# Moving a LayerNorm's 1/std broadcast within a hand-ordered state-space layer

## The chip, the cores and the metric

The kernel runs on one NeuronCore of a Trainium2 chip. The core has five engines that run side by side, each through its own list of instructions: TensorE (PE, matmuls and transposes), VectorE (DVE), ScalarE (ACT), GpSimd (POOL) and SyncE (SP, which here only issues DMAs). The metric is the device time of one execution in microseconds (us). Before the change it is 11733.97 us, the median of three runs (11728.79 to 11737.78).

## What is computed

The input is 4 images of 192 channels and 128 x 128 pixels. Layer 1 of the network (called `layer0` in the code) is a fractional-Fourier convolution block; the change does not touch it. Layer 2 (`layer1` in the code) is a GroupNorm followed by a selective state-space block over the 16384 pixels of each image as one sequence. Cut to what matters:

```python
mu  = jnp.mean(seq, -1, keepdims=True)                      # over the 192 channels of one token
var = jnp.mean(jnp.square(seq - mu), -1, keepdims=True)
seq = (seq - mu) * lax.rsqrt(var + LN_EPS) * ln_g + ln_b    # LayerNorm
xs, z = jnp.split(jnp.einsum('blc,ec->ble', seq, in_proj_w), 2, axis=-1)
u  = silu(causal depthwise conv(xs) + conv_b)
dt, Bm, Cm = jnp.split(jnp.einsum('bld,kd->blk', u, x_proj_w), ...)
dt = jax.nn.softplus(jnp.einsum('blr,dr->bld', dt, dt_proj_w) + dt_proj_b)
def step(hcar, inp):                                        # over tokens, 384 x 16 states
    hnew = hcar * jnp.exp(dt_t[..., None] * A) + (dt_t * u_t)[..., None] * B_t[:, None, :]
    y_t  = jnp.sum(hnew * C_t[:, None, :], axis=-1)
out = jnp.einsum('bld,cd->blc', (y + u * Dp) * silu(z), out_proj_w)
```

## The kernel before

**Tiling.** Layer 2 cuts the sequences into 128 chunks of 512 tokens. In a chunk the 384 inner channels are three blocks `j` of 128 partitions, and the 16 states of each are taken two at a time, so a chunk is 24 groups, `k = 0..23`, with `j = k // 8` and `sg = k % 8`. A group has two scans: one `tensor_tensor_scan` on VectorE (L868) runs the recurrence of one state over 512 tokens. Below, "scan 22.1" is the second scan of group 22.

**What a scan needs.** The decay `exp(dt*A)` comes from ScalarE (`da` or `op`, L799). The input `dt*u*B` comes from one of three places: from VectorE itself (`product`, L819), for some groups from GpSimd (`inputs`, L827: `db`), and for `sg == 6` from ScalarE and TensorE (`scale_pair` L843, then four transposes in `turned_back`, L854). GpSimd multiplies each group's result by C (`hc`, L881) and TensorE sums those into `py` (L894), three groups later (`LAG = 3`). At the end of a block `j`, ScalarE copies `py` out (`evacuate`, L903), TensorE turns it (`turn`, L918, four transposes into a PSUM tile `pf`), and VectorE multiplies by `silu(z)` (`gate`, L923, which writes `yg`).

**The front end of later chunks.** While the 24 groups of chunk n run, the generator `front(n + 2)` computes what a later chunk needs: GroupNorm and LayerNorm, `in_proj`, the convolution, silu, `x_proj`, softplus. It is started at group 14 of chunk n and advanced once per group, so two fronts are under way at a time. Each `yield` ends its work in that group. A bare `yield` resumes at the front's fixed place in the next group, ahead of the scans. `yield MID` hands the following piece to the list that is resumed between the two scans of the same group (`between`), and `yield LATE` to the list that is resumed after both.

**The part that is changed** is LayerNorm's scaling of `s`, the 192 x 512 values kept as `[96, 2, 512]`. The variance of the 512 tokens ends up as `rs`, 128 partitions x 4. ScalarE takes the root (L640), VectorE the reciprocal (L643, after the scans of group 20), TensorE turns `rs` into 4 rows (L646, group 21, a PSUM tile `rt`), ScalarE copies them to `rows` (L649, between the scans of group 21), four matmuls with the selector `sel` spread them over 96 partitions (L653, group 22, a PSUM tile `rb`), and VectorE multiplies `s` by that (L657, after the scans of group 22). `in_proj` of the scaled `s` (L663) begins in group 23.

**Order.** The whole layer is recorded under `tc.manual_schedule()`, so each engine executes in the order in which the code issues its instructions. Per group the order is: the finishing of the previous chunk, the gate, `turned_back`, `sums`, the fronts' step, `turn`, `inputs`, the scans with what stands between them, and then the late pieces. The groups concerned, on TensorE: group 20 has the sums, one `in_proj` of `z` for the older front (two matmuls, L663) and the turn; group 21 a `turned_back`, the sums, L646 and a second `turned_back`; group 22 the sums, another `in_proj` of `z`, L653; group 23 the sums and the first `in_proj` of the scaled `s`.

**Buffers.** The PSUM tiles of the fronts, of `turn` and of `turned` all come from one pool of three (`psum()`); a new tile waits until the last reader of the one whose place it takes is done. The `da` tiles come from a pool of four, `h` of three, `hc` of five, `db` of two.

```python
yield MID        # rows = copy(rt)            between the scans of group 21
yield            # rb: selector matmuls       at the front's place in group 22
yield LATE       # s *= rb                    after the scans of group 22
```

Of the kernel before, what the change touches and what calls it, by code (L numbers as in the profile page):

```python
# [42 lines left out]
def _bc(ap, axis, n):  # L43

    a = ap.unsqueeze(axis)
    shape = list(a.shape)
    shape[axis] = n
    return a.to_broadcast(shape)
# [455 lines left out]
def layer1(tc, xmid, out, st2, w, n_tok=S * S):  # L504
# [11 lines left out]
    MID, LATE = "mid", "late"  # L516
    with ExitStack() as ctx:
# [68 lines left out]
        def psum():  # L586
            return ps1.tile([128, 512], F32, name="ps")
# [6 lines left out]
        def load_x(i):  # L594
            b, ch = divmod(i, NCHUNK)
            xm = xp.tile([CH, 2, T], F32, name="xm")
            nc.sync.dma_start(
                out=xm, in_=xmid[b][:, ch * T : (ch + 1) * T].rearrange("(t p) f -> p t f", p=CH)
            )
            got[i]["xm"] = xm  # L600

        def front(i):
# [38 lines left out]
            yield  # L641
            yield LATE
            nc.vector.reciprocal(rs, rs)  # L643
            yield
            rt = psum()
            nc.tensor.transpose(rt[0:4, 0:128], rs, ident)  # L646
            yield MID
            rows = tp.tile([4, 128], F32, name="rows")
            nc.scalar.copy(rows, rt[0:4, 0:128])  # L649
            yield  # L650
            rb = psum()
            for q in range(4):
                nc.tensor.matmul(  # L653
                    rb[0:CH, q * 128 : (q + 1) * 128], sel[:, q, :], rows, start=True, stop=True
                )
            yield LATE
            nc.vector.tensor_tensor(s, s, _bc(rb[0:CH], 1, 2), ALU.mult)  # L657
            yield

# [110 lines left out]
        def load_bc(i, sg):  # L770

            t = bcp.tile([128, 2, G, T], F32, name="bc")
            nc.sync.dma_start(
                out=t, in_=got[i]["dbc"][:, sg * G : (sg + 1) * G, :].partition_broadcast(128)
            )
            got[i]["bc", sg] = t

        def dtu_copy(n, j):

            g = got[n]  # L780
            g["dp"] = psd.tile([128, T], F32, name="dp")
            nc.scalar.copy(g["dp"], g["dtu"][j])  # L782
# [19 lines left out]
        def early(i):  # L802

            if i < len(own):
                decay(own[i], scp.tile([128, T], F32, name="da"))

        def decay_there(s):

            if s < len(states) and s not in turns:
                decay(s, psa.tile([128, T], F32, name="op"))  # L810

        def product(s):


            if s in turns and states[s][1] % NG != BY_PE:
                n, k, q = states[s]
                g = got[n]
                dbs[s] = psa.tile([128, T], F32, name="op")
                nc.vector.tensor_tensor(dbs[s], g["dp"], g["bc", k % NG][:, 0, q, :], ALU.mult)  # L819

        def inputs(n, k):

            if by_pool(k):
                g = got[n]
                j, sg = divmod(k, NG)
                db = g["db", k] = scp.tile([128, G, T], F32, name="db", bufs=2)
                nc.gpsimd.tensor_tensor(db, _bc(g["dtu"][j], 1, G), g["bc", sg][:, 0], ALU.mult)  # L827
# [19 lines left out]
        def turned_back(at):  # L847

            if at < len(states) and states[at][1] % NG == BY_PE:
                n, k, q = states[at]  # L850
                db = dbs[at] = psa.tile([128, T], F32, name="op")
                t = got[n].pop(("dbT", k // NG, q))
                for blk in range(T // 128):
                    nc.tensor.transpose(db[:, blk * 128 : (blk + 1) * 128], t[:, blk, :], ident)  # L854
# [29 lines left out]
        def sums(n, k):  # L884

            g = got[n]
            j, sg = divmod(k, NG)
            if sg == 0:
                g["py", j] = psy.tile([128, T // 128, 128], F32, name="py")
            py, hc = g["py", j], g.pop(("hc", k))  # L890
            for q in range(G):
                for blk in range(T // 128):
                    first = sg == 0 and q == 0 and blk == 0
                    nc.tensor.matmul(  # L894
                        py[:, blk, :], hc[:, q, blk * 128 : (blk + 1) * 128], ident, start=first,
                        stop=sg == NG - 1 and q == G - 1 and blk == T // 128 - 1,
                        is_transpose=True, skip_group_check=True,
                    )

        def evacuate(n, j):  # L900
            g = got[n]
            yt = g["yt", j] = op.tile([128, T // 128, 128], F32, name="yt")
            nc.scalar.copy(yt, g["py", j])  # L903
# [16 lines left out]
        def gate(n, j):  # L920
            g = got[n]
            yg = g["yg", j] = op.tile([128, T], F32, name="yg", bufs=3)
            nc.vector.tensor_mul(yg, g["pf", j], g["zs"][j])  # L923
# [24 lines left out]
        def start_front(n):  # L948
            if n < total:
                fronts.append(front(n))  # L950

        def step(works, parts):

            for f in list(works):
                got_on = next(f, f)
                if got_on is f:
                    works.remove(f)
                elif got_on is not None:
                    parts[got_on].append(f)

        def go_on(fs):
            for f in fs:
                next(f, None)

        with tc.manual_schedule():
            for i in range(min(2, total)):
                load_x(i)
            for _ in front(0):
                pass
            for sg in range(NG):  # L970
                load_bc(0, sg)
            dtu_copy(0, 0)
            inputs(*order[1])
            for at in range(AHEAD):
                early(at)
            for s in range(2):
                product(s)
            decay_there(2)


            start_front(1)
            for _ in range(NGR - FRONT):
                parts = {MID: [], LATE: []}
                step(fronts, parts)
                go_on(parts[MID] + parts[LATE])
            tails = []
            for pos, (n, k) in enumerate(order):
                j, sg = divmod(k, NG)
                if k == FRONT:
                    start_front(n + 2)  # L990
                if k == NGR - 2 and n + 1 < total:
                    assert len(fronts) == 1 + (n + 2 < total), fronts
                parts = {MID: [], LATE: []}
                step(tails, parts)

                before = n - (j == 0), (j - 1) % NJ
                if pos >= NG and sg == LAG + 3:
                    gate(*before)
                if sg == BY_PE - 1:
                    turned_back(G * (pos + 1))  # L1000
                if pos >= LAG and sg != LAG:
                    sums(*order[pos - LAG])
                if k == EARLY or sg == LAG - 1 and j < NJ - 1:
                    turned(n, NJ - 1 if k == EARLY else j)
                if sg == NG - 3 and pos + 3 < len(order):
                    m, q = order[pos + 3]
                    dtu_copy(m, q // NG)
                step(fronts, parts)
                if pos >= NG and sg == LAG + 1:
                    turn(*before)  # L1010
                if pos + 2 < len(order):
                    inputs(*order[pos + 2])

                def between():
                    go_on(parts[MID])
                    if sg == LAG and j < NJ - 1:
                        scale_pair(n, j)

                scans(pos, n, k, between)
                if pos >= NG and sg == LAG - 1:  # L1020
                    evacuate(*before)
                go_on(parts[LATE])
                if k == EARLY:
                    scale_pair(n, NJ - 1)
                if pos >= LAG and sg == LAG:
                    sums(*order[pos - LAG])
                    add_skip(n, j)
                if k == LAG + 3 and n:
                    tails.append(finish(n - 1))
                if k == LAG + 8 and n + 2 < total:  # L1030
                    load_x(n + 2)
                if k >= NGR - BCL and n + 1 < total:
                    load_bc(n + 1, k - (NGR - BCL))
                if k < NG - BCL and n:
                    load_bc(n, k + BCL)
            for at in order[-LAG:]:
                sums(*at)
            evacuate(total - 1, NJ - 1)
            turn(total - 1, NJ - 1)
            gate(total - 1, NJ - 1)  # L1040
            for _ in finish(total - 1):
                pass
# [139 lines left out]
```

## Time and profile before

| what | value |
|---|---|
| median of three runs | 11733.97 us |
| the profiled execution | 11752.54 us, its span 11750.5 us |
| VectorE busy | 10759.5 us, 92% of the span |
| GpSimd busy | 10087.8 us, 86% |
| TensorE matmuls busy | 9994.0 us, 85% |
| ScalarE busy | 8606.6 us, 73% |
| L868, all scans | 6144 instructions of about 1271 ns |
| L657, scaling of s | 128 instructions of 1217 ns, 225.6 us idle before them |

The page of the profile has for each engine its busy time and its share of the span, then the same in 40 slices of the span, then the groups of instructions by source line: how many, how long one takes, and for how long the engine stood idle just before them and what ended that. Layer 2 begins about 1500 us into the span and takes the rest. The profiled execution is 18.6 us longer than the median of the plain runs, 0.16%.

### The profile page before, as it was taken

The page shows a single profiled execution, that of the slowest core. Times are in us where ns is not written, and L with a number is a line of the kernel's source. Part 1 is how long each engine was busy: PE and PEld are TensorE (multiplying, and loading weights), DVE is VectorE, ACT ScalarE, POOL GpSimd, SP SyncE. Part 2 cuts the span into 40 slices and gives each one's busy share as a digit, 9 for nine tenths or more (in the row PEclk, how much of TensorE's full clock was granted, in tenths as well). Part 3 has the DMA queues.
Part 4 walks back from the last instruction along what each step waited for, and adds up shares of the span by engine and source line. Part 5 has one row for each costly group of instructions (what it writes and reads, how often), then busy time and mean ns, then how long its engine had stood idle before and what let it go on. Part 6 is the DMA issues. An engine that isn't in the chain of part 4 may idle for free.

```text
span 11750.5 us, 153548 instructions
## 1 busy us (share of the span) xinstructions
PE 9994.0 (85%) x50570; PEld 6788.1 (58%) x50570; DVE 10759.5 (92%) x11584; ACT 8606.6 (73%) x14436; POOL 10087.8 (86%) x4598
## 2 busy tenths in 40 slices
PE   4777888888888888888888888888888888888887
PEld 2444456666666666666666666666666666666665
DVE  5565579999999999999999999999999999999999
ACT  2322178788888788788788788788888878878876
POOL 0000089999999999999999999999999999999999
PEclk8888689999999999999999999999999999999998
DMA  8887633433433443443443443443343343344343
GB/s 208 209 223 194 185 109 113 124 114 111 124 117 108 124 123 103 126 125 100 126 124 102 123 124 106 120 124 108 117 124 113 113 124 115 111 124 118 108 124 97
DMA packets 1339384, 1494.09 MB, mean 127 GB/s; under 512 B 903473, under 2 KB 954358, under 8 KB 1338070
## 3 DMA queue, kind: packets, MB, share of 16 engines
q1 hardware_dynamic: 1318102, 1421.34, 42.0%
q0 software_dynamic: 13312, 50.34, 1.3%
q10 hardware_dynamic: 7168, 12.59, 0.3%
q8 instruction: 398, 6.52, 0.2%
q14 instruction: 404, 3.31, 0.1%
HBM read 1325.19 MB, written 155.32 MB: 126 GB/s over the span
## 4 chain that ended last, share of the span: by engine, by line
DVE 42%; ACT 20%; PE 19%; issue 12%; DMA 4%; POOL 1%; DVEq 1%; SPq 0%; ACTq 0%; POOLq 0%
DVE h L868 29%; DVE op L819 10%; PE py L894 5%; ACT da L799 5%; ACT op L799 4%; PE ps L663 3%; ACT dbT L843 2%; ACT L799 2%; PE pr L471 2%; PE py L908 2%; ACT dt L744 1%; DMA xt<-in_x 1%; ACT L744 1%; DMA bc<-dbc 1%; PE ps L653 1%
## 5 line engine op out<-in xcount | busy, mean ns | idle before, releaser
L881 POOL TENSOR_TENSOR hc<-h,bc 128x1024 f32<-128x1024 f32 x3072 | 7198.0, 2366 | 244.7 <-DVE h L868 218.7
L868 DVE TENSOR_TENSOR_SCAN h<-da,carry,op 128x512 f32<-128x512 f32 x3968 | 4945.7, 1271 | 2.3 <-issue 0.5
L894 PE MATMUL py<-ident,hc 128*128 128x128 f32 x24576 | 3482.6, 291 | 680.1 <-ACT yt L903 653.5
L894 PEld LDWEIGHTS py<-ident,hc 128*128 128x128 f32 x24576 | 3049.8, 151 | 1585.1 <-issue 754.3
L799 ACT ACTIVATE da<-dt,c_A_log 128x512 f32<-128x512 f32 x4096 | 2813.7, 721 | 558.2 <-DVE h L868 551.9
L868 DVE TENSOR_TENSOR_SCAN h<-op,carry,db 128x512 f32<-128x512 f32 x1984 | 2522.3, 1271 | 84.2 <-issue 82.2
L827 POOL TENSOR_TENSOR db<-dtu,bc 128x1024 f32<-128x1024 f32 x1024 | 2419.6, 2363 | 7.9 <-DMA bc<-dbc 7.8
L819 DVE TENSOR_TENSOR op<-dp,bc 128x512 f32<-128x512 f32 x3328 | 2252.5, 677 | 32.9 <-ACT dp L782 32.9
L799 ACT ACTIVATE op<-dt,c_A_log 128x512 f32<-128x512 f32 x2048 | 1398.8, 689 | 979.0 <-DVE h L868 978.8
L663 PE MATMUL ps<-s,c_wiT 96*128 96x512 f32 x3072 | 1468.5, 601 | 38.4 <-DVE s L657 38.4
L681 PE MATMUL ps<-xs,dcw 128*128 128x512 f32 x3072 | 1424.3, 592 | 0.2 <-ACT xs L676 0.2
L799 ACT ACT_TABLE_LOAD x636 | 816.0, 1283 | 11.5 <-DVE h L868 0.3
L843 ACT ACTIVATE dbT<-ps,bT 128x128 f32<-128x128 f32 x3072 | 822.0, 371 | 0.0
L932 PE MATMUL ps<-yg,c_woT 128*96 128x512 f32 x1536 | 711.8, 599 | 112.6 <-DVE xm L938 112.6
L663 PEld LDWEIGHTS ps<-s,c_wiT 96*128 96x128 f32 x3072 | 531.3, 193 | 445.9 <-issue 376.7
L681 PEld LDWEIGHTS ps<-xs,dcw 128*128 128x128 f32 x3072 | 533.1, 190 | 432.5 <-issue 432.1
L477 POOL DMA_DIRECT2D xmid<-xt x64 | 42.9, 671 | 782.6 <-DVE xt L475 775.9
L908 PE MATMUL py<-ddp,u 128*128 128x128 f32 x3072 | 536.0, 333 | 0.0
L633 PE MATMUL ps<-ones,xs 96*128 96x1 f32 x2048 | 346.2, 299 | 199.0 <-ACT dt L744 194.2
L932 PEld LDWEIGHTS ps<-yg,c_woT 128*96 128x96 f32 x1536 | 240.2, 163 | 472.0 <-issue 318.9
L908 PEld LDWEIGHTS py<-ddp,u 128*128 128x128 f32 x3072 | 511.1, 251 | 0.0
L748 POOL TENSOR_TENSOR dtu<-dt,u 128x512 f32<-128x512 f32 x384 | 476.6, 1269 | 30.1 <-ACT dt L744 30.1
(172 smaller groups left out, 10267.7 us busy)
## 6 DMA issues: line engine op xcount, KB each, us to landing
bc<-dbc SPq DMA_DIRECT2D x1024, 1024.0 KB, 5.9
xt<-in_x SPq DMA_DIRECT2D x192, 768.0 KB, 9.4
xmid<-xt POOLq DMA_DIRECT2D x64, 768.0 KB, 7.2
xm<-xmid SPq DMA_DIRECT2D x128, 384.0 KB, 3.6
carry<-h SPq DMA_DIRECT2D x3072, 1.0 KB, 1.9
out<-xm SPq DMA_DIRECT2D x128, 384.0 KB, 3.3
d<-x ACTq DMA_DIRECT2D x64, 192.0 KB, 7.8
df<-u SPq DMA_DIRECT2D x16, 512.0 KB, 4.9
```

What stands on the lines that cost most here:

```text
L663: nc.tensor.matmul(pp, wiT[:, t, m * 128 : (m + 1) * 128], s[:, t, :], start=t == 0, stop=t == 1)
L681: nc.tensor.matmul(pc, dcw[:, j, k, :], xs[:, j, k : k + T], start=k == 0, stop=k == 3)
L748: nc.gpsimd.tensor_tensor(dtu[j], dt[j], u[j], ALU.mult)
L799: nc.scalar.activation(da, got[n]["dt"][j], AF.Exp, scale=A[:, j, st : st + 1])
L819: nc.vector.tensor_tensor(dbs[s], g["dp"], g["bc", k % NG][:, 0, q, :], ALU.mult)
L827: nc.gpsimd.tensor_tensor(db, _bc(g["dtu"][j], 1, G), g["bc", sg][:, 0], ALU.mult)
L843: nc.scalar.activation(t[:, blk, :], g["tu", j][:, blk, :], AF.Identity, scale=g["bT"][:, blk, q : q + 1])
L868: nc.vector.tensor_tensor_scan(h[:, q, :], das.pop(s), dbs.pop(s) if db is None else db[:, q, :], 0.0 if ch == 0 else g["before"][:, j, st ...
L881: nc.gpsimd.tensor_tensor(hc, h, g["bc", sg][:, 1], ALU.mult)
L894: nc.tensor.matmul(py[:, blk, :], hc[:, q, blk * 128 : (blk + 1) * 128], ident, start=first, stop=sg == NG - 1 and q == G - 1 and blk == T ...
L908: nc.tensor.matmul(got[n]["py", j][:, blk, :], got[n]["u"][j][:, blk * 128 : (blk + 1) * 128], ddp[:, j, :], start=False, stop=False, skip ...
L932: nc.tensor.matmul(po[0:CH], woT[:, j, t * CH : (t + 1) * CH], g["yg", j], start=j == 0, stop=j == NJ - 1,)
```

## The change

Three statements of `front` move, and the helper `go_on` learns to pass a generator on. The transpose of `rs` (L646) is issued right after the reciprocal, after the scans of group 20, instead of at the front's place in group 21. The copy to `rows` stays between the scans of group 21. The four selector matmuls (L653) are issued after the scans of group 21 instead of in group 22. The scaling of `s` (L657) is issued between the two scans of group 22 instead of after them. To let a piece that ran between the scans be followed by one after the scans of the same group, `go_on` now looks at what the generator yields and puts it into the list named. No instruction is added or removed.

```diff
             nc.vector.reciprocal(rs, rs)
-            yield
             rt = psum()
             nc.tensor.transpose(rt[0:4, 0:128], rs, ident)
+            yield
             yield MID
             rows = tp.tile([4, 128], F32, name="rows")
             nc.scalar.copy(rows, rt[0:4, 0:128])
-            yield
+            yield LATE
             rb = psum()
             for q in range(4):
                 nc.tensor.matmul(
                     rb[0:CH, q * 128 : (q + 1) * 128], sel[:, q, :], rows, start=True, stop=True
                 )
-            yield LATE
+            yield
+            yield MID
             nc.vector.tensor_tensor(s, s, _bc(rb[0:CH], 1, 2), ALU.mult)
             yield
...
-        def go_on(fs):
-            for f in fs:
-                next(f, None)
+        def go_on(parts, part):
+
+            for f in parts[part]:
+                got_on = next(f, None)
+                if got_on is not None:
+                    parts[got_on].append(f)
...
-                go_on(parts[MID] + parts[LATE])
+                go_on(parts, MID)
+                go_on(parts, LATE)
...
                 def between():
-                    go_on(parts[MID])
+                    go_on(parts, MID)
...
-                go_on(parts[LATE])
+                go_on(parts, LATE)
```

## The prediction

> **What bounds the kernel now.** I read first the windows view of 399 us in the middle of layer 2 (five chunks of about 79.8), then the waits view of the same stretch, then the timeline of two chunks around L657.
>
> ```profile
> core 0: us, PE busy (x) PEld busy (x) DVE busy (x) ACT busy (x) POOL busy (x), PEclk, DMA share, GB/s
> 6000.00:6399.00 399.00, 347.37 (x1845) 242.32 (x1844) 386.73 (x410) 322.31 (x545) 389.83 (x176) 0.94 0.40 117
> ```
>
> VectorE is busy 386.73 of 399 us, GpSimd 389.83. So VectorE needs 77.3 us a chunk and GpSimd 78.0, and both are nearly full. VectorE's 12.3 us of idle time are few and known:
>
> ```profile
> ACT rows L649 <- PE ps L646: 8.7, 5, 2.6
> POOL hc L881 <- DVE h L868: 8.7, 18, 1.2
> DVE s L657 <- PE ps L653: 8.5, 5, 2.3
> DVE h L868 <- issue: 3.6, 6, 0.7
> ```
>
> VectorE waits 8.5 us in five chunks for the selector matmuls, 1.7 a chunk, and 0.7 a chunk at scan 15.0 (by its place behind ScalarE's decay). GpSimd's 8.7 us are waits for scans: they follow VectorE's stall. The stall of single chunks, from their timeline rows, runs 1.07, 2.28, 1.49, 2.28, 1.60 and repeats. A chunk with the small one, VectorE and TensorE:
>
> ```profile
> 6061.76 0.17 DVE L643 RECIPROCAL rs<-rs 128x4 f32<-128x4 f32 x1
> 6061.85 2.43 DVE L868 TENSOR_TENSOR_SCAN h<-da,carry,op 128x512 f32<-128x512 f32 x2
> 6064.18 0.67 DVE L923 TENSOR_TENSOR yg<-ps,zs 128x512 f32<-128x512 f32 x1
> 6064.77 2.45 DVE L868 TENSOR_TENSOR_SCAN h<-da,carry,op 128x512 f32<-128x512 f32 x2
> 6068.28 1.22 DVE L657 TENSOR_TENSOR s<-s,ps 96x1024 f32<-96x1024 f32 x1 [1.07 <-PE ps L653]
> ```
>
> ```profile
> 6062.16 0.60 PE L918 MATMUL ps<-ident,yt 128*128 128x128 f32 x4
> 6062.60 0.60 PE L854 MATMUL op<-ident,dbT 128*128 128x128 f32 x4
> 6063.03 1.04 PE L894 MATMUL py<-ident,hc 128*128 128x128 f32 x8
> 6063.91 0.27 PE L646 MATMUL ps<-ident,rs 128*4 128x128 f32 x1
> 6064.02 0.60 PE L854 MATMUL op<-ident,dbT 128*128 128x128 f32 x4
> 6064.45 1.04 PE L894 MATMUL py<-ident,hc 128*128 128x128 f32 x8
> 6065.33 1.88 PE L663 MATMUL ps<-s,c_wiT 96*128 96x512 f32 x4
> 6067.14 1.11 PE L653 MATMUL ps<-rows,sel 4*96 4x128 f32 x8
> ```
>
> TensorE is not idle here: it is behind. VectorE had the reciprocal at 6061.93; TensorE came to L646 only at 6063.91, because the turn, four transposes and eight sums stood ahead. Then eight more sums and an `in_proj` of z stood ahead of L653. Nothing that L657 needs takes long; it stands in a queue. A chunk with the large stall, and the granted clock (column PEclk) before each of the two:
>
> ```profile
> 6148.74 1.22 DVE L657 TENSOR_TENSOR s<-s,ps 96x1024 f32<-96x1024 f32 x1 [2.28 <-PE ps L653]
> ```
>
> ```profile
> 6142.62 0.60 PE L918 MATMUL ps<-ident,yt 128*128 128x128 f32 x4
> ```
>
> ```profile
> 6048.67:6058.87 10.20, 8.93 (x42) 0.50 0.06 2
> 6134.00:6140.90 6.90, 5.09 (x25) 0.51 0.33 95
> ```
>
> I measure from the start b of scan 22.0: 6064.77, and 6143.87 in the other chunk. The turn starts at b-2.61 in the one, b-1.25 in the other: TensorE had half its clock at another time.
>
> **What the Trainium skill says.** "Trainium Architecture — The Big Picture", section "Inside one NeuronCore": each engine has its own instruction stream, and the engines meet only at semaphores; so a matmul's place in TensorE's list counts as much as its inputs. The trace agrees: 1.98 us from reciprocal to L646. "Perfetto Trace Analysis", section "Identifying Dependency Chains": an instruction that waits on several engines may get extra semaphore instructions ahead of it. The built program has this at the moved L653 (below). "TensorE: Matmul & The Clock Gate", section "What's actually happening": the gate halves the clock by a free-running window of 3413 ns. The trace agrees (0.50 in 10.20 us, about three windows), and it explains why the stall depends on how a chunk falls against the windows.
>
> **The change, part by part.** Instructions and their number stay; the lists of ScalarE, GpSimd and SP (with its DMAs) are the same in both built programs. Only TensorE and VectorE are reordered.
>
> 1. *L646 after the turn.* It now has only the turn ahead: 4 transposes at 0.44 back to back, so b-2.17 or b-0.81. The reciprocal ends at b-2.84, so TensorE doesn't wait. It delays the first L854 by 0.11 us; that one ended at about b-0.2 in the bad chunk and feeds scan 22.0: some 0.1 left, cost nothing.
> 2. *`rows` (L649)* follows L646 by 0.31 and takes 0.25. ScalarE, which waited there 1.7 us a chunk, is free after its copy of `dp` at b-1.5. `rows` ends by b-1.2 or b-0.25.
> 3. *L653 at the end of group 21.* Behind L646 come L854, sums, L854: 0.11 + 0.44 + 0.87 + 0.44 = 1.86, so TensorE could start L653 at b-0.31 or b+1.05. But in the built program `rb` takes the PSUM place of `pf` and waits also for the gate of group 22 (L923), which ends at b+0.08; before, an `in_proj` had this wait. So L653 starts at b+0.15 or b+1.05. It takes 1.11. Behind it wait the sums and the `in_proj` of z; nobody needs these soon (silu of z is in group 23).
> 4. *L657 between the scans.* It can start 0.04 after L653: b+1.30 or b+2.20. Back to back it would start 1.18 after scan 22.0. Remaining delay: 0.12 or 1.02. The other classes of chunk (turn at b-2.19, b-2.08) give 0.12 and 0.19. Mean over 1.07, 2.28, 1.49, 2.28, 1.60: (0.12 + 1.02 + 0.12 + 1.02 + 0.19) / 5 = 0.49. Before, L657 could have started 2.36 after b; its delay there was the stall plus 0.09 of overlap, mean 1.83. Gain 1.34 us a chunk.
> 5. *Scan 22.1 comes later*, by L657 and what is left of the stall: it ends at b+3.70 or b+4.60 where it was b+2.45. GpSimd's `hc` of group 22 started at about b+3.6, so it idles 0.3 or 1.2 there. In total, 79.8 - 1.34 = 78.5 us a chunk leave GpSimd 0.5 of slack. It must run some 0.2 us later against VectorE than now; scan 9.0 then finds its `db` (on average 0.46 ahead, at the least 0.03) late in some chunks. I take 0.1 a chunk for this, between 0 and 0.5.
> 6. *ScalarE's `da` for scan 2.1* waits for scan 22.1 (pool of four) and stood at b+2.69; it now stands at b+3.74. Behind it: two table loads, two silus, a copy, then the decay for scan 1.0, 4.65 later, 0.67 long: ready at b+9.1. Scan 1.0 comes at b+9.5. The slack of 2.1 us shrinks to about 0.46 in both classes, but holds.
>
> Sum: 1.34 - 0.1 = 1.24 us, for 126 chunks (fronts 2 to 127; the first two run ahead of the loop): 157 us. The profiled execution (11752.54, span 11750.5) would become about 11,595; from the median of the plain runs, 11733.97 - 157 = 11,577 us.
>
> **Rivals.**
>
> *GpSimd becomes the bound* (12%). For: 78.0 us a chunk of work. If its backlog cannot grow, its idle time at `hc` of group 22 (mean 0.66) and some 0.4 elsewhere stay: 79.06 us a chunk, a gain of 0.74 x 126 = 93: 11,641 us. Against: `h` has three buffers, and every scan outside `db` groups has on average over 1.6 us of slack to GpSimd.
>
> *The clock decides* (13%). The windows are 3.413 us; 23 of them are 78.50, just the new length of a chunk, so the chunks could stay at one place against them. Always the bad place: gain 1.83 - 1.02 = 0.81, 102 us: 11,632. Always the good one: 1.71, 215 us: 11,519.
>
> *No change* (6%): TensorE, later against VectorE by about 0.9 us after group 23, reaches the turn and L854 of group 6 late in the chunks where they have only 0.04 to 0.3 us to spare, and gives the stall back there. Against: TensorE waits 2.40 us for ScalarE's `yt` in between, which absorbs it. 11,734.
>
> *Slower* (9%): ScalarE takes over at scan 1.0. If step 6 is 2.3 us worse than I have it (TensorE late with z for the silus, since L653 now goes first; a decay waiting for an `op` place), scan 1.0 waits 2.3 - 0.46 = 1.84 us each chunk against 1.34 won: +0.5 x 126 = 63: 11,797 us. It decides from 1.8 us beyond my estimate on. For: ScalarE has the two table loads just there, and scans 15.0 and 17.0 already have under 0.2 us to spare. Against: z is ready at b+3.95 or 4.85, before its silu at b+5.65 or 6.55.
>
> **Numbers.** The forecast itself has 60%. The range reaches from always-good (11,519) to a little past GpSimd's bound: 11,515 to 11,660. A measurement of this kernel can tell 0.2% (23 us) from no change. Faster by more: 60 + 12 + 13 = 85%, less 1 for a residue; within 0.2%: 6%; slower: 9 + 1 = 10%.
>
> **What would show it.** In the profile after: L657's idle time down from 225.6 us to about 50 (L653 still its releaser); `rows` waiting for L646 down from 221.8 to below 100; GpSimd's idle before `hc` down from 244.7 to some 60 to 90; L653 starting right behind the gate in three of five chunks; a short new wait of scan 9.0 for `db`. Wrong, if VectorE shows a new wait before scan 1.0 or scan 6.0, or if L653 starts later than b+1.1.

## The result, and the profile after

The changed kernel takes 11587.34 us in the median of four runs (11581.39 to 11593.71), the kernel before 11732.83 in the median of four (11728.79 to 11737.78): ratio 0.9876, 95% interval 0.9859 to 0.9893. It is faster by 1.2%. The profiled execution takes 11590.68 us, its span 11588.6, so the span lost 161.9 us. The changed kernel's lines are numbered one higher from L645 on: L645 is the transpose of `rs`, L653 the selector matmuls as before, L658 the scaling.

The windows view of the same stretch of layer 2 (for each of the engines PE, PEld, DVE, ACT and POOL its busy us and, in brackets, its instructions, then the granted clock and the DMA figures; PEld is TensorE loading weights), and the waits view of it (who waited for whom: us in total, times, longest):

```profile
6000.00:6399.00 399.00, 345.11 (x1881) 239.12 (x1880) 393.15 (x418) 328.58 (x556) 396.14 (x179) 0.96 0.42 123
```

```profile
DVE h L869 <- issue: 3.3, 5, 0.7
POOL hc L882 <- DVE h L869: 2.9, 5, 0.6
ACT rows L649 <- PE ps L645: 2.6, 5, 0.5
DVE s L658 <- PE ps L653: 2.5, 5, 0.5
```

VectorE is busy 393.15 of 399 us where it was 386.73, and its wait for the selector matmuls fell from 8.5 to 2.5 us. The waits of `rows` and of GpSimd fell from 8.7 us each to 2.6 and 2.9. Over the whole run L658 has 71.8 us of waits where L657 had 225.6. The wait of 0.7 at scan 15.0 is as it was.

One chunk, VectorE, TensorE and GpSimd from the timeline (start, length, engine, line), with the scaling of the next three chunks below it:

```profile
6068.27 0.16 DVE L643 RECIPROCAL rs<-rs 128x4 f32<-128x4 f32 x1
...
6070.69 0.66 DVE L924 TENSOR_TENSOR yg<-ps,zs 128x512 f32<-128x512 f32 x1
6071.27 1.26 DVE L869 TENSOR_TENSOR_SCAN h<-da,carry,op 128x512 f32<-128x512 f32 x1
6073.05 1.22 DVE L658 TENSOR_TENSOR s<-s,ps 96x1024 f32<-96x1024 f32 x1 [0.51 <-PE ps L653]
6074.19 1.27 DVE L869 TENSOR_TENSOR_SCAN h<-da,carry,op 128x512 f32<-128x512 f32 x1
...
6151.55 1.22 DVE L658 TENSOR_TENSOR s<-s,ps 96x1024 f32<-96x1024 f32 x1 [0.50 <-PE ps L653]
...
6230.07 1.22 DVE L658 TENSOR_TENSOR s<-s,ps 96x1024 f32<-96x1024 f32 x1 [0.51 <-PE ps L653]
...
6308.57 1.22 DVE L658 TENSOR_TENSOR s<-s,ps 96x1024 f32<-96x1024 f32 x1 [0.50 <-PE ps L653]
```

```profile
6069.52 0.60 PE L919 MATMUL ps<-ident,yt 128*128 128x128 f32 x4
6069.95 0.27 PE L645 MATMUL ps<-ident,rs 128*4 128x128 f32 x1
6070.06 0.60 PE L855 MATMUL op<-ident,dbT 128*128 128x128 f32 x4
6070.50 1.04 PE L895 MATMUL py<-ident,hc 128*128 128x128 f32 x8
6071.37 0.60 PE L855 MATMUL op<-ident,dbT 128*128 128x128 f32 x4
6071.90 1.11 PE L653 MATMUL ps<-rows,sel 4*96 4x128 f32 x8
```

```profile
6072.69 2.36 POOL L882 TENSOR_TENSOR hc<-h,bc 128x1024 f32<-128x1024 f32 x1
6075.63 2.36 POOL L882 TENSOR_TENSOR hc<-h,bc 128x1024 f32<-128x1024 f32 x1 [0.59 <-DVE h L869]
```

TensorE still comes to L645 1.5 us after the reciprocal is done, but L653 now follows 1.95 us behind L645 instead of 3.23. The scaling is asked for right after one scan and still waits, 0.5 us. GpSimd's only idle time in the chunk is ahead of `hc` of group 22, whose second scan comes later.

What nobody would read from the sum alone is in the four rows of L658. Each has the same stall, and the starts are 78.50, 78.52 and 78.50 us apart. Before, the stall ran through five values. From the sixth chunk on, the median distance is 78.507 us, and 119 of 122 distances lie within 0.15 us of it. The granted clock shows what goes with this (in a row: the stretch, its length, TensorE's busy time and matmuls, the granted clock, the DMA share and GB/s):

```profile
6060.35:6067.18 6.83, 5.66 (x28) 0.50 0.18 40
6138.86:6145.69 6.83, 5.65 (x27) 0.50 0.19 42
6217.37:6224.20 6.83, 5.66 (x28) 0.50 0.20 53
6295.88:6302.71 6.83, 5.66 (x27) 0.50 0.18 51
```

In each chunk TensorE's clock is halved in the same place, from 10.9 to 4.1 us before scan 22.0. The changes of clock in the trace stand on a grid of 3.4133 us (a halved stretch is two steps of it, and 69 steps lie between the first and the last row), and 23 of its steps are 78.507 us. The chunk is as long as 23 windows of the clock gate. (Before, five chunks took 399.35 us, and 117 windows are 399.36.)

### The profile page after: what moved, and what is told of

The parts are those of the page before. It is cut to its first block, busy times and chain, and to the rows that moved or that the text cites. A ratio compares the mean times of both kernels' runs of the same rounds, so it can differ in the third digit from the quotient of the medians.

```text
span 11588.6 us, 153548 instructions
## 1 busy us (share of the span) xinstructions
PE 9794.3 (85%) x50570; PEld 6612.4 (57%) x50570; DVE 10751.8 (93%) x11584; ACT 8608.4 (74%) x14436; POOL 10072.1 (87%) x4598
## 4 chain that ended last, share of the span: by engine, by line
DVE 32%; ACT 23%; PE 22%; issue 14%; POOL 6%; DMA 2%; DVEq 0%; SPq 0%; POOLq 0%; ACTq 0%
DVE h L869 23%; DVE op L820 7%; PE py L895 6%; ACT da L800 6%; POOL hc L882 4%; ACT op L800 4%; ACT L800 2%; ACT dbT L844 2%; PE py L909 2%; PE ps L664 2%; PE pr L471 2%; ACT dt L745 1%; POOL db L828 1%; PE ps L682 1%; PE op L855 1%
## 5 line engine op out<-in xcount | busy, mean ns | idle before, releaser
L882 POOL TENSOR_TENSOR hc<-h,bc 128x1024 f32<-128x1024 f32 x3072 | 7195.2, 2374 | 95.7 <-DVE h L869 93.7
L895 PE MATMUL py<-ident,hc 128*128 128x128 f32 x24576 | 3346.1, 283 | 604.5 <-ACT yt L904 368.3
L895 PEld LDWEIGHTS py<-ident,hc 128*128 128x128 f32 x24576 | 2941.5, 147 | 1589.7 <-issue 701.4
L633 PE MATMUL ps<-ones,xs 96*128 96x1 f32 x2048 | 292.7, 273 | 287.2 <-ACT dt L745 282.3
L909 PEld LDWEIGHTS py<-ddp,u 128*128 128x128 f32 x3072 | 487.6, 241 | 0.0
```

Of the source, the lines that this page charges most:

```text
L882: nc.gpsimd.tensor_tensor(hc, h, g["bc", sg][:, 1], ALU.mult)
L895: nc.tensor.matmul(py[:, blk, :], hc[:, q, blk * 128 : (blk + 1) * 128], ident, start=first, stop=sg == NG - 1 and q == G - 1 and blk == T ...
L909: nc.tensor.matmul(got[n]["py", j][:, blk, :], got[n]["u"][j][:, blk * 128 : (blk + 1) * 128], ddp[:, j, :], start=False, stop=False, skip ...
```

## The experiments

Two questions were open: which of the three moves brings the gain, and whether the 0.50 us that is left is a fixed delay or is set by the clock windows. In this table the length of a chunk is the mean distance between the starts of consecutive scalings of `s`, from the sixth on; the stall is the mean idle time of VectorE before them in 100 chunks from the middle.

| run | what it is | chunk, us | stall, us | ratio to before (95%) |
|---|---|---|---|---|
| before | | 79.85 | 1.75 | 1 |
| the change | three moves | 78.51 | 0.53 | 0.9876 (0.9859 to 0.9893) |
| rt_only | L646 earlier | 79.84 | 1.73 | 0.9999 (0.9990 to 1.0007) |
| s_only | scaling between the scans | 81.29 | 3.24 | 1.0159 (1.0144 to 1.0174) |
| rb_only | L653 earlier | 77.98 | 0.00 | 0.9806 (0.9791 to 0.9821) |
| s_late | L646 and L653 earlier | 77.98 | 0.00 | 0.9803 (0.9789 to 0.9818) |
| after_r | the change and one reciprocal | 78.51 | 0.33 | 0.9860 (0.9845 to 0.9874) |
| s_late_r | s_late and one reciprocal | 78.17 | 0.00 | 0.9824 (0.9807 to 0.9840) |
| after_r3 | the change and three reciprocals | 79.31 | 0.34 | 0.9947 (0.9931 to 0.9964) |
| after_03 | the change and one product | 80.25 | 0.43 | 1.0027 (1.0016 to 1.0038) |
| after_06 | the change and two products | 82.15 | 0.21 | 1.0257 (1.0239 to 1.0274) |

In the runs beside the experiments the kernel before took 11751.5 to 11752.8 us in the median, not 11732.83, so the ratios compare and the times do not. The chunk and the stall come from the profiled execution of a run; that of after_03 was the longest of seven (11811.92 us, their median 11780.10), so its chunk is too long for its ratio.

### s_late: without the move of the scaling

```diff
             yield
-            yield MID
+            yield LATE
             nc.vector.tensor_tensor(s, s, _bc(rb[0:CH], 1, 2), ALU.mult)
```

> The changed kernel, but the scaling of s (L658) issued after both scans of group 22, as before. Theory Q (the gain is the selector matmuls' place in TensorE's queue; the move of the scaling costs): s is then asked for 2.36 us after the start of scan 22.0, and in the changed kernel its input was there at 1.77: no stall is left before L658, the chunk goes from 78.51 to 78.0 to 78.2 us (VectorE's work and its wait at scan 15.0, GpSimd's 78.0), so about 11,530 to 11,550 us. Rival R1 (all three moves are needed): as slow as before in part, above 11,600. Rival R2 (GpSimd holds the chunk at 78.5): 11,580 to 11,595, with VectorE waiting for db or h.

It takes 11521.14 us, ratio 0.9803, faster than both kernels; the time lies a little below the 11,530 to 11,550 us that theory Q expected, and the chunk just below its 78.0. Its timeline of VectorE, and its windows view:

```profile
6041.30 0.66 DVE L924 TENSOR_TENSOR yg<-ps,zs 128x512 f32<-128x512 f32 x1
6041.88 2.44 DVE L869 TENSOR_TENSOR_SCAN h<-da,carry,op 128x512 f32<-128x512 f32 x2
6044.24 1.19 DVE L658 TENSOR_TENSOR s<-s,ps 96x1024 f32<-96x1024 f32 x1
```

```profile
6000.00:6399.00 399.00, 353.57 (x1886) 246.81 (x1885) 395.28 (x420) 328.93 (x558) 398.38 (x180) 0.94 0.39 118
```

No wait stands before the scaling. L653 starts at 6042.43 in this chunk and takes 1.11 us; its result is there 0.7 us before VectorE asks for it. So theory Q has the mechanism right, and R1 falls. GpSimd, 398.38 us busy out of 399, is now full, with the chunk at 77.98 and not at 78.5: R2 falls too. GpSimd, together with VectorE's 0.7 us at scan 15.0, leaves little to win by more moves of this kind.

### rb_only: the selector matmuls alone

```diff
             nc.scalar.copy(rows, rt[0:4, 0:128])
-            yield
+            yield LATE
             rb = psum()
...
+            yield
             yield LATE
             nc.vector.tensor_tensor(s, s, _bc(rb[0:CH], 1, 2), ALU.mult)
```

Here `go_on` is the changed one, and L646 stays in group 21.

> Only the selector matmuls (L653) are moved to the end of group 21; the transpose of rs (L646) stands in group 21 and the scaling after the scans of group 22, as before. Theory Q: the transpose is ready at the same time for the copy to rows, give or take 0.3 us, since the queue ahead of L653 is the same; within 10 us of s_late, 11,530 to 11,555 us. Rival R1 (the early transpose is what makes it work): the copy to rows waits for L646 as before (about 220 us in all) and the gain is less by about that, above 11,620.

```profile
L658 DVE TENSOR_TENSOR s<-s,ps 96x1024 f32<-96x1024 f32 x128 | 152.6, 1192 | 5.7 <-PE ps L653 5.7
```

This is the row of the scaling in the groups by line: busy time, mean ns, idle time before it and what ended that. The stall is gone but for 5.7 us before the first two scalings. The time is 11524.35 us, the ratio 0.9806: the same as s_late, and like it a little faster than the range expected. `rows` waits 223.2 us for L646, as before the change, and that costs nothing. So the half of R1 that expected a loss from this wait falls: ScalarE had time to spare there.

### rt_only and s_only: the other two moves alone

rt_only moves L646 behind the reciprocal and nothing else (the first two marked lines of the change's diff); s_only turns the `yield LATE` before the scaling into `yield MID` in the kernel before.

> The kernel before with only the transpose of rs (L645) moved behind the reciprocal; selector matmuls in group 22, scaling after its scans. Theory Q: the queue ahead of the selector matmuls has the same work in another order, so the stall stays near 1.76 us a chunk and the ratio is 0.998 to 1.002, although the copy to rows no longer waits long for TensorE (its wait falls from 222 us to under 110). Rival R1 (the early transpose carries the gain): ratio under 0.995.

> The kernel before with only the scaling moved between the scans of group 22. Theory Q: the scaling is asked for 1.18 us earlier and its input comes no earlier, so the stall grows by about 1.2 us to 3.0 a chunk: some 155 us more, ratio 1.010 to 1.016. Rival R3 (the move between the scans helps by itself, since scan 22.1 then hides part of the wait): ratio 1.000 or below.

The rows of the scaling in the groups by line, rt_only first:

```profile
L657 DVE TENSOR_TENSOR s<-s,ps 96x1024 f32<-96x1024 f32 x128 | 155.9, 1218 | 224.9 <-PE ps L653 224.9
```

```profile
L657 DVE TENSOR_TENSOR s<-s,ps 96x1024 f32<-96x1024 f32 x128 | 155.8, 1218 | 412.7 <-PE ps L653 412.7
```

The early transpose alone changes nothing (224.9 us against 225.6), though `rows` waits only 62.6 us for L645. The move of the scaling alone costs 1.6%: its stall goes up by 1.49 us a chunk, somewhat more than the 1.2 by which it is asked for earlier. So the whole gain is the place of L653, and the change gave a part of it back by asking for the result one scan sooner.

### after_03 and after_06: extra work that was mis-sized

```diff
+                if k == 3:
+                    nc.vector.tensor_tensor(junk, junk, junk, ALU.mult)
```

`junk` is a scratch tile of 128x240 ones; nothing reads it. after_06 has two of these.

> The changed kernel with one more VectorE instruction a chunk, a product of 128x240 in place on a scratch tile after the scans of group 3, worth some 0.30 us. Theory L (the chunk is locked to 23 windows of the clock gate, 78.507 us; the stall before L658 makes up the rest): the chunk stays at 78.50 to 78.52, the stall falls from 0.50 to about 0.2, the time stays within 8 us of the changed kernel. Rival N (the stall is a fixed delay of TensorE's queue): the chunk grows to 78.80, the stall stays 0.5, the time grows by 0.3 x 128 = 38 us.

> The same with two such instructions, some 0.60 us. Theory L: the stall can fall only to about 0.03, so 0.47 is absorbed and at least 0.13 shows: the lock breaks, the stall differs from chunk to chunk as before the change, its mean between 0.05 and 0.4, chunk 78.6 to 79.0. Rival N: 79.10, stall 0.5 in each chunk, time up by 77 us.

The product takes 1.88 us on average, not 0.30, so both runs missed what they were made for: neither theory said 1.0027 and 1.0257. The timelines of VectorE and GpSimd in after_03:

```profile
6023.66 1.46 DVE L1031 TENSOR_TENSOR junk<-junk 128x240 f32<-128x240 f32 x1
6025.05 1.27 DVE L871 TENSOR_TENSOR_SCAN h<-op,carry,db 128x512 f32<-128x512 f32 x1
```

```profile
6020.18 2.35 POOL L830 TENSOR_TENSOR db<-dtu,bc 128x1024 f32<-128x1024 f32 x1
6022.48 4.86 POOL L884 TENSOR_TENSOR hc<-h,bc 128x1024 f32<-128x1024 f32 x2
```

The product ends at 6025.12, shortly after GpSimd's first `hc` of this row (half of 4.86 us: until about 6024.9). This is so in every chunk: the 128 products last 1.19 to 4.64 us, and each ends 0.26 to 0.27 us after an instruction of GpSimd has ended. So the trace shows that the product waits for GpSimd. The Trainium skill, "GPSIMD Engine Reference", section "1. Specifications", says that GpSimd's SBUF interfaces are shared with VectorE and contend with its instructions that have two SBUF inputs. `junk` has two; the kernel's own product L819 of twice the size takes one from PSUM and needs 0.68 beside the same GpSimd. And in layer 1, where GpSimd is busy for only 93 of 1400 us, a product of 128x360 in place with two inputs in SBUF (L359) takes 0.53. The trace agrees with the page: the long times come only where both are there, two inputs in SBUF and a busy GpSimd. No run changes only the place of one input.

### after_r, s_late_r and after_r3: the same with a reciprocal

```diff
-                    nc.vector.tensor_tensor(junk, junk, junk, ALU.mult)
+                    nc.vector.reciprocal(junk, junk)
```

with `junk` 128x32. after_r3 has three.

> The changed kernel with one more VectorE instruction a chunk after the scans of group 3: a reciprocal of 128x32 in place on a scratch tile, worth some 0.27 us (the product of the run after_03 took 1.87 us instead of 0.30, so it could not tell). Theory L (chunk locked to 23 windows of the clock gate, 78.507 us): chunk 78.50 to 78.53, stall before the scaling down from 0.50 to about 0.23, GpSimd's idle time before hc of group 22 down by as much or unchanged, ratio to before 0.987 to 0.989, as the changed kernel's 0.9876. Rival N (the stall is a fixed delay): chunk 78.78, stall 0.50, ratio 0.990 to 0.991.

> The control: the same extra reciprocal in s_late, where no stall is left that could give way. Both theories: the chunk grows from 77.98 by about 0.27 to 78.25 us, ratio to before from 0.9803 to about 0.983. If it stays at 77.98, the reciprocal is hidden in another wait and the run after_r tells nothing.

The timeline of VectorE in after_r:

```profile
6069.60 1.22 DVE L660 TENSOR_TENSOR s<-s,ps 96x1024 f32<-96x1024 f32 x1 [0.31 <-PE ps L655]
...
6087.25 0.32 DVE L1031 RECIPROCAL junk<-junk 128x32 f32<-128x32 f32 x1
...
6148.11 1.22 DVE L660 TENSOR_TENSOR s<-s,ps 96x1024 f32<-96x1024 f32 x1 [0.30 <-PE ps L655]
```

The distance is again 78.51 us (median 78.507), with the reciprocal in it, and the stall went from 0.50 to 0.31 in most chunks. The ratio, 0.9860, is that of the change. In s_late_r, where no stall can give way, the same instruction lengthens the chunk from 77.98 to 78.17 us and the ratio goes from 0.9803 to 0.9824 (the intervals of these two overlap; the lengths of the chunks tell them apart). So the chunk of the changed kernel does not change with 0.2 us more of VectorE's work: it is held at 78.507. Theory L holds, N falls.

> The changed kernel with three of the reciprocals of the run after_r after the scans of group 3. One cost about 0.18 us a chunk where nothing gave way (s_late_r against s_late) and took 0.20 off the stall in after_r, so three are some 0.55 to 0.6 us. Theory L (lock to 23 clock windows): the stall can give up at most about 0.45, so the lock breaks: chunk 78.6 to 78.9 us in the mean, the stall no longer the same in each chunk, ratio to before 0.987 to 0.991. Rival N (fixed delay, nothing gives way): chunk 79.08, stall 0.50 in each chunk, ratio 0.994.

Three reciprocals in a row on one tile take 1.02 us from start to start, not 0.6, so the expected 78.6 to 78.9 was missed, and the ratio would have suited N. The stalls decide; rows from the timeline of after_r3:

```profile
6195.20 1.22 DVE L660 TENSOR_TENSOR s<-s,ps 96x1024 f32<-96x1024 f32 x1 [0.90 <-PE ps L655]
...
6274.49 1.22 DVE L660 TENSOR_TENSOR s<-s,ps 96x1024 f32<-96x1024 f32 x1 [0.32 <-PE ps L655]
...
6353.54 1.22 DVE L660 TENSOR_TENSOR s<-s,ps 96x1024 f32<-96x1024 f32 x1
```

The stall is no longer the same: 0.90, 0.32, 0.08 and 0.08 in turn (the last are below what the view marks). Four chunks mostly take 317.44 us, which is 93 windows. The lock to 23 windows is gone and another, over four chunks, is in its place.

## Why the prediction was right, point by point

- *What bounds it: a queue, not an input.* Right. rb_only shows it alone: earlier in TensorE's list by the sums and one `in_proj`, L653 removes all of VectorE's stall.
- *Steps 1 and 2, the transpose and `rows`.* Right in time (L645 at b-1.32; `rows` waits 69.8 us in all) and in cost (no wait before scan 22.0). They also bring nothing, which the prediction didn't say: the run rt_only shows it.
- *Step 3.* L653 was to start at the gate's end, b+0.15, in three of five chunks. It starts at b+0.63 in all of the usual ones: TensorE is the later one, and the gate is done 0.55 us before. The wait itself is there (the trace has a semaphore instruction ahead of L653 in each of 126 chunks), but it is over before it matters. It does set the start in after_r3, in the chunks with a stall of 0.08 us: the selector matmuls start there at b+0.23, 0.15 us after the gate. A kernel without that wait was not tried.
- *Step 4, the size.* The remaining delay was to be 0.12 or 1.02 us by the class of the chunk, 0.49 in the mean. It is 1.77 - 1.18 = 0.59 in every usual chunk, so the step gained 1.83 - 0.59 = 1.24 us and not 1.34. The chunk as a whole lost 79.85 - 78.51 = 1.34 us, where 1.24 was predicted. That these are so near is luck in part: some 0.1 us came from elsewhere (VectorE's busy time fell by 7.7 us in all, 0.06 a chunk, and small waits got shorter), which the prediction did not count, and the 0.59 has another reason than its mean of 0.49. The prediction averaged the five classes of the kernel before; these are gone with the length of the chunk that made them. The cause stood among the rivals, as "the clock decides", and the prediction had seen that 23 windows are as long as the new chunk; it gave this case 13% and only its two ends as results. The chunks did come to rest at one place against the windows, but at the place where the stall makes the chunk 23 windows long.
- *Step 5, GpSimd.* It idles 0.57 us at `hc` of group 22, predicted 0.66 in the mean. The wait of scan 9.0 for `db` is there, 0.02 us a chunk; 0.1 was too much.
- *Step 6, ScalarE.* The decay is ready 0.38 us before scan 1.0, predicted 0.46. The rival "slower" would have needed the decay some 1.8 us later than estimated.
- *The rival "no change"* (TensorE late at group 6): the turn there is done 1.77 us before its gate in nearly every chunk, where two of five had 0.04 to 0.14 before. In one of those two the clock is halved from 20.9 to 24.3 us after the preceding scan 22.0, and the turn starts at 26.5; after the change no halved stretch lies there.
- *The sum.* 157 us were predicted from the profile (1.24 x 126 is 156); the spans differ by 161.9, the medians by 145.5 (the interval of the ratio is 0.17% to either side, 20 us). Of what was named for the profile after, the wait of `rows` came out below 100 us; L658's idle time is 71.8 us and not about 50, and GpSimd's before `hc` 95.7 and not 60 to 90.

What the prediction did not ask is whether each of the three moves earns its place. By its own numbers, L653 would have been done at b+1.26 or b+2.16, ahead of the old place of the scaling at b+2.36. That the move of the scaling gives time away (0.7%: 0.9876 against 0.9803) could have been read from them.

## What to carry to other kernels

Where an engine waits for a small matmul, look at what stands ahead of that matmul in TensorE's list before looking at its inputs; moving it ahead of work that nobody needs soon can be the whole gain. Do not move the consumer forward in the same step: count the producer's new finish against the consumer's old place first. And measure each move by itself, since two that look like one idea had opposite signs here.

## What the runs showed of the hardware that was not expected

**A loop can lock to the clock gate's windows.** The Trainium skill, "TensorE: Matmul & The Clock Gate", section "What's actually happening", says that the window is free-running, 3413 ns. The runs add what this did to a loop in which VectorE waits for TensorE once a chunk. It settled, for most of layer 2, at a whole number of windows: 23 for one chunk (78.507 us) in the changed kernel and in after_r, 117 for five chunks before and in rt_only, 143 for six in s_only (488.1 us), 93 for four in after_r3. In after_03 and after_06, where the products wait for GpSimd too, no such length shows. In the changed kernel the loop comes back after a disturbance, here the first chunk of an image:

```profile
4031.88 1.22 DVE L658 TENSOR_TENSOR s<-s,ps 96x1024 f32<-96x1024 f32 x1 [0.50 <-PE ps L653]
...
4110.07 1.22 DVE L658 TENSOR_TENSOR s<-s,ps 96x1024 f32<-96x1024 f32 x1 [0.96 <-PE ps L653]
...
4188.64 1.22 DVE L658 TENSOR_TENSOR s<-s,ps 96x1024 f32<-96x1024 f32 x1 [0.74 <-PE ps L653]
...
4267.27 1.22 DVE L658 TENSOR_TENSOR s<-s,ps 96x1024 f32<-96x1024 f32 x1 [0.62 <-PE ps L653]
```

The distance of 78.19 us is followed by 78.57, 78.63, 78.57, 78.54 and 78.52, while the stall runs 0.96, 0.74, 0.62, 0.57, 0.53, 0.52 and the end of the halved clock moves from 3.4 to 4.1 us before scan 22.0. This says why it holds: a chunk that is too short lets the windows fall later in the next one, TensorE comes later, and the stall makes up for it. That the windows are the cause is read from these lengths and from this return; no run took the halving away. While it holds, 0.2 us of more work in the loop cost nothing (after_r), so an experiment that adds so little can show no effect where the work is not free; less work was not tried. In s_late, which has no stall to give, the halved clock wanders from chunk to chunk.

**Half the clock without an idle window.** The same section has the halved state follow an idle window. The window ahead of the first halved stretch shown above (columns as there):

```profile
6056.94:6060.35 3.41, 1.49 (x14) 1.00 0.04 0
```

TensorE is busy for 1.49 of 3.41 us there, and in the halved stretch itself for 5.66 of 6.83. From 1700 to 11300 us the changed kernel has 129 halved stretches, and in the window ahead of each TensorE is busy for 37% or more. So here the measurement decides: no idle window was needed. Which windows are followed by half the clock stays open, since the busy share alone doesn't tell: up to 78% came before a halving, and other windows with 48% did not bring one.

**A VectorE product with both inputs in SBUF waited for GpSimd.** Beside a GpSimd that is nearly always busy, a product of 128x240 with both inputs in SBUF took 1.88 us in the mean and ended with GpSimd's instructions; one of 128x512 with an input in PSUM took 0.68, and a reciprocal of 128x32, with its one input in SBUF, 0.32.
